# Third layer of a recurrent model: the readout turned back block by block inside the recurrence, and the last block in two halves

## The chip, the core and the metric

The kernel runs on one core of one Trainium2 chip. The metric is the device time of one execution in microseconds (us), as the median of several runs. A core has five engines that the profile names: PE (TensorE, the matrix engine, with PEld for its weight loads), DVE (VectorE), ACT (ScalarE), POOL (GpSimd) and SP (SyncE, which here only issues transfers). Each takes its instructions from a queue of its own, in the order in which the built kernel has them.

## The reference, cut to what matters

The model has four layers on 4 sequences of 256 tokens, 128 features wide. The change lies in the attention part of the third layer (index L2), a gated delta rule with a rotation: 16 heads, each with a state of 2 x 16. Beside it the same layer has a mixture of eight experts; the layer's output is x + attention + silu(experts).

```python
def step(S, inp):
    ct, st, kt, vt, bt = inp
    S0, S1 = (S[:, :, 0], S[:, :, 1])
    Sd = jnp.stack([ct[..., None] * S0 + st[..., None] * S1, -st[..., None] * S0 + ct[..., None] * S1], axis=2)
    pred = jnp.einsum('bhsd,bhd->bhs', Sd, kt)
    Sn = Sd + bt[:, :, None, None] * (vt - pred)[..., None] * kt[:, :, None, :]
    return (Sn, Sn)
...
_, Ys = jax.lax.scan(step, S0, xs)
Y = jnp.moveaxis(Ys, 0, 1)
retrieved = jnp.einsum('blhsd,blhd->blhs', Y, Q) * sel_C_gate[..., None]
y = retrieved.reshape(b, l, h * 2) @ readout_w
```

A group norm over the sequence, a silu gate and an output projection follow. The norm needs all 256 tokens of a sequence, so nothing behind it can begin before the last token's `retrieved`.

## The kernel before

**Layout.** The recurrence is computed without the rotation: keys and values are turned beforehand by the accumulated angle, so that a step only decays and updates, and what is read from the states is turned back afterwards with `cosp` and `sinp`. The partitions are state component x sequence x head (2 x 64 = 128 rows), and each row holds 16 numbers of state. The tokens come in NT = 8 blocks of 128 columns, each of NC = 16 chunks of CH = 8 tokens. Rows 0 to 63 and 64 to 127 are the two components of the same sequence and head.

**The recurrence** is the loop at the end of `scan2`: 128 steps n = 16 i + c (block i, chunk c), each four VectorE operations in a chain (L1664 product, L1667 sum, L1670 product, L1675 sum). A step gives the state at the chunk's end and the weights `w` of its 8 tokens. Every second step ScalarE copies two chunks' coefficients into the step's state tile (`bring`, L1644, three steps ahead); L1675 of a step waits for that copy.

**The states of all tokens** of a block are made from `w` by the generator `states(i, w)`, in six stages: load kt (SP); load qt, spread the decays into mz (L1601, ScalarE) and clear its first column; kt * w (L1606, POOL, with two small operations for the state carried in, L1611 and L1612); the scan over the block's tokens for 16 numbers at a time (L1615, VectorE, 128x2048), the copy of its last state for the next block (`last`, L1617, ScalarE) and the product with qt (L1618, POOL); 16 matmuls that sum over the 16 numbers (L1623, `read`, PE); the copy of the result to `o` (L1625, ScalarE). The tiles qt and mz exist once, kt twice.

**What sets the order.** The loop advances these generators by hand, after fixed chunks c: `turns` maps c to how many blocks back the advanced generator lies (c = 4 and 12 this block, c = 1 and 11 the block before, c = 3 and 7 the one before that). After the loop the last two generators are drained, so that the scan, the product and the reads of block 7 all stand behind the recurrence. After each step the loop also advances `beside`, the mixture of experts of the same layer (`experts2`): per sequence a router (L1068 to L1074), and per half of it eight experts, each with a gathered input `xs` (L1083, POOL), four transposes (L1090, PE), a copy `xin` (L1092, ScalarE), matmuls up (L1112) and down (L1101, L1102) with two ScalarE operations on `h` between (L1113, L1114), and a shared expert (L1122 to L1128); the result is turned (gT, L1130; PE's transposes in a helper at L125) and written out as `g` (L1134). The tile framework's scheduler then fixes each engine's order: it places every instruction into one queue per engine, so that expert work and recurrence work interleave in fixed order. Transposes take PSUM buffers of the tag "tr", which in this stage is the same as the experts' "mm" (three buffers).

**After the recurrence** `retrieve2` turns `o` (eight PE transposes, two 512-wide copies), multiplies and adds on 128x512 tiles (six VectorE and two POOL operations with cosp, sinp and outg, which is the gate sigmoid(sel_C) over |Q|), and transposes back to `retT`. `out2` then runs for the four sequences: 16 matmuls L1724 from retT, copies, statistics, the norm, the gate with sz (L1750, L1751) and the projection (L1760); it adds resid and g, loaded from DRAM by `layer2` (L1016, L1017).

**The gates** are computed by `gates2` before the recurrence: cosp and sinp, outg, and the coefficients, on 128x512 tiles on VectorE (`mul`, L1230) and POOL (`mulp`, L1231).

Of the kernel before, what the change touches and what calls it, by code (L numbers as in the profile page):

```python
# [10 lines left out]
F32 = mybir.dt.float32  # L11
# [4 lines left out]
ALU = mybir.AluOpType  # L16
AX = mybir.AxisListType
# [3 lines left out]
P = 128  # L21
NB = 4
T = 1024
NT = 8
# [906 lines left out]
def layer2(k, W, x_all, eps5, ps, banks, x3, whole, last, I, first):  # L931
# [4 lines left out]
    nc, tc = k.nc, k.tc  # L936
    tokens = lambda b: slice(b * NT, (b + 1) * NT)
    with tc.tile_pool(name="l2", bufs=1) as keep, tc.tile_pool(name="l2dram", bufs=1, space=DRAM) as dram:
        wide = lambda name: dram.tile([P, NB * NT, D], F32, tag=name, name=name)

        xd, rd, gd, xr = wide("xd"), wide("rd"), wide("gd"), wide("xr")
        szd = dram.tile([P, 2, NB * T], F32, tag="szd", name="szd")

        kd = dram.tile([NT, NB, 16, 16, P], F32, tag="kd", name="kd")
        qd = dram.tile([NT, NB, 16, 16, P], F32, tag="qd", name="qd")
        small = lambda name, shape=(P, 512): keep.tile(list(shape), F32, tag=name, name=name)
        cosp, sinp, outg = small("cosp"), small("sinp"), small("outg")
        coef = {name: small(name) for name in ("bias0", "bias1", "scale", "decay")}
        o = small("o", (P, T))
        late = ExitStack()  # L950
        with tc.tile_pool(name="l2g", bufs=1, side="right") as gp:
            raw = {
                "V": gp.tile([P, 32, 32], F32, tag="V", name="V"),
                "G": gp.tile([P, 7, 32, 16], F32, tag="G", name="G"),
                "N": gp.tile([P, 2, 32, 16], F32, tag="N", name="N"),
            }
            with tc.tile_pool(name="l2p", bufs=1) as p1, tc.tile_pool(name="l2pd", bufs=2) as p2:
                xn = p1.tile([P, NB * NT, D], F32, tag="xn", name="xn")

                def norm(b):  # L960

# [12 lines left out]
            banks.close()  # L974
            ps = PsumTags(banks, tc, {"mm": 3, "tr": "mm", "o": 2, "st": 2, "A": 1}, "ps2s")
            f1 = late.enter_context(tc.tile_pool(name="l2f", bufs=1))
            f2 = late.enter_context(tc.tile_pool(name="l2fd", bufs=2))
            experts = experts2(k, W, f1, f2, ps, xd, gd)
            early = {}
            with tc.tile_pool(name="l2m", bufs=1) as mp, tc.tile_pool(name="l2y", bufs=2) as yp:  # L980
                grams = grams2(k, f1, mp, yp, ps, kd, early)

                def beside():

                    while True:
# [12 lines left out]

        def behind_tables():
            room.close()  # L1000
            pre = room.enter_context(tc.tile_pool(name="l2pre", bufs=1, side="right"))
            for b in range(NB):
                szs.append(pre.tile([P, 2, T], F32, tag=f"sz{b}", name="sz"))
                nc.sync.dma_start(out=szs[b], in_=szd[:, :, b * T : (b + 1) * T])

        with late, tc.tile_pool(name="l2s1", bufs=1) as p1, tc.tile_pool(name="l2s", bufs=2) as p2, \
                tc.tile_pool(name="l2sd", bufs=2, space=DRAM) as dram2:
            scan2(k, p1, p2, ps, dram2, kd, qd, coef, o, experts, tp1, tp2, behind_tables, early)
        banks.close()
        ps = PsumTags(banks, tc, {"mm": 4, "tr": 2, "o": 2}, "ps2o")  # L1010
        with room, tc.tile_pool(name="l2o", bufs=NB) as p4, tc.tile_pool(name="l2x", bufs=2) as p2, \
                tc.tile_pool(name="l2r", bufs=1) as p1, tc.tile_pool(name="w3", bufs=1) as w3:
            parts = []
            for b in range(NB):
                resid, g = (p4.tile([P, NT, D], F32, tag=tag, name=tag) for tag in ("resid", "g"))
                nc.sync.dma_start(out=resid, in_=rd[:, tokens(b), :])  # L1016
                nc.sync.dma_start(out=g, in_=gd[:, tokens(b), :])  # L1017
                parts.append((resid, g))
            W3 = load3(k, w3, I)
            turned = prepare3(k, t3, W3, ps)  # L1020
            retT = p1.tile([P, T], F32, tag="retT", name="retT")
            retrieve2(k, p1, ps, o, cosp, sinp, outg, retT)
            done = []
            ends = [
                out2(k, W, p4, p2, ps, b, retT, szs[b], *parts[b], eps5, xr[:, tokens(b), :], x3[:, tokens(b), :], done)
                for b in range(NB)
            ]
            begin = None
            for n in range(2 * NB):
                for b in range(NB):  # L1030
                    if 0 <= n - b:
                        next(ends[b], None)
                        next(turned, None)
                        if done and begin is None:
                            begin = begin_first(k, W3, p1, ps, done[0], eps5, first)
                        if begin:
                            next(begin, None)
            drain(turned)
        return W3
# [182 lines left out]
def gates2(k, W, mp, ps, raw, cosp, sinp, outg, coef, beside, decays):  # L1222
# [152 lines left out]
    v.tensor_tensor(a1, a1, w, ALU.add)  # L1375
    mul(a0, a0, bv)
    mul(a1, a1, bv)

    for name, src in (("bias0", a0), ("bias1", a1)):
        k.transpose_tiles(ps, "tr", block(src), coef[name])  # L1380
# [166 lines left out]
        yield ktd, kdd  # L1547


def scan2(k, p1, p2, ps, dram, kd, qd, coef, o, beside, tp1, tp2, behind_tables, early):  # L1550

# [33 lines left out]
    def states(i, w):  # L1585
# [36 lines left out]
        for d in range(16):  # L1622
            nc.tensor.matmul(po, k.ident, hist[:, d, :], start=(d == 0), stop=(d == 15))  # L1623
        yield
        nc.scalar.copy(o[:, at], po)  # L1625
        yield

    def load(i):
        if i < NT:
# [17 lines left out]
            )  # L1647


    turns = {4: 0, 12: 0, 1: 1, 11: 1, 3: 2, 7: 2}  # L1650
    blocks, made_of = {}, {}
    load(0)
    bring(0)
# [1 line left out]
    for i in range(NT):  # L1655
# [4 lines left out]
        for c in range(NC):  # L1660
# [14 lines left out]
            v.tensor_reduce(then[:, 0:16, CH], step, AX.X, ALU.add)  # L1675
            next(beside, None)
            if c == 0:
                made_of[i] = states(i, w)
            if c in turns and i - turns[c] in made_of:
                next(made_of[i - turns[c]])  # L1680
            for _ in range(2 if i == 0 else 1):
                if len(made) < min(4, i + 3):
                    table()
# [5 lines left out]
    for i in (NT - 2, NT - 1):  # L1689
        drain(made_of[i])  # L1690
    drain(beside)


def retrieve2(k, p2, ps, o, cosp, sinp, outg, retT):

    nc = k.nc
    O = p2.tile([P, 8, 2, 64], F32, tag="O", name="O")
    k.transpose_tiles(ps, "tr", [o[:, (n % 2 * 4 + n // 2) * P :][:, 0:P] for n in range(NT)], O.rearrange("p a s c -> p (a s c)"))
    wide = lambda a: a.rearrange("p (a c) -> p a c", c=64)
    o0, o1 = O[:, :, 0, :], O[:, :, 1, :]  # L1700
    ret = p2.tile([P, 8, 64, 2], F32, tag="ret", name="ret")
    for s, (x, y, op) in enumerate(((o0, o1, ALU.add), (o1, o0, ALU.subtract))):
        a = p2.tile([P, 8, 64], F32, tag="a", name="a")
        u = p2.tile([P, 8, 64], F32, tag="u", name="u")
        nc.vector.tensor_tensor(a, x, wide(cosp), ALU.mult)
        nc.gpsimd.tensor_tensor(u, y, wide(sinp), ALU.mult)
        nc.vector.tensor_tensor(a, a, u, op)
        nc.vector.tensor_tensor(ret[:, :, :, s], a, wide(outg), ALU.mult)
    tiles = [ret[:, 2 * tt4 + half].rearrange("p c s -> p (c s)") for half in range(2) for tt4 in range(4)]
    k.transpose_tiles(ps, "tr", tiles, retT)  # L1710


def out2(k, W, p2, px, ps, b, retT, sz, resid, g, eps5, x_from, x_to, done):
# [680 lines left out]
```

## Time and profile before

| what | value |
|---|---|
| median of 3 runs | 3140.76 us (3139.37 to 3149.32) |
| the profiled execution | 3140.11 us, span 3138.4 us |
| granted TensorE clock, mean | 0.741 |
| busy, whole span | PE 69%, DVE 72%, ACT 50%, POOL 40% |
| the recurrence (L1664 to L1675) | 1652.1 to 1994.84 us |
| its last block, first step | 1967.01 us |
| experts' last ScalarE operation (g, L1134) | 1914.94 us |
| scans L1615, blocks 0 to 7, start | 1730.98, 1818.36, 1852.80, 1895.15, 1928.29, 1956.81, 1984.76, 1998.88 us |
| first product of `out2` (L1724) | 2024.59 us |

All times inside the profile are microseconds from the start of the span. A timeline line gives start, duration, engine, source line, operation, the tile written and the tiles read with their shapes, and in brackets how long the engine had been idle before and who released it. A waits line gives the instruction that waited, the one that it waited for, the total, how often and the longest. The windows view gives the busy time of each engine in each stretch. A source line can be that of a helper (L115, L117 and L125 are the copies and transposes of `transpose_tiles`).

### The profile page before, as it was taken

To read this page: it belongs to the slowest core of one execution; us is meant where nothing else is said; L and a number is where in the kernel's file an instruction comes from. 1 tells how busy PE (TensorE), PEld (TensorE's weight loads), DVE (VectorE), ACT (ScalarE), POOL (GpSimd) and SP (SyncE) were. 2 spreads that over 40 slices of the span, in tenths; PEclk is the share of its full clock that TensorE was granted. 3 is DMA by queue.
4 is the path that set the end of the run, shared out by engine and by line. 5 is a ranking of instruction groups with operands and counts; after the bars stand their busy time and mean duration, and the time that the engine had idled before them with its cause. 6 is when DMAs were issued, how large, how long until landed. Compare 5 with 4: busy or idle time off the path is not lost. (4 is left out here: it accounts for less than half of the span.)

```text
span 3138.4 us, 48108 instructions
## 1 busy us (share of the span) xinstructions
PE 2160.2 (69%) x17200; PEld 1281.2 (41%) x17201; DVE 2262.5 (72%) x5474; ACT 1565.8 (50%) x3350; POOL 1258.3 (40%) x1154
## 2 busy tenths in 40 slices
PE   5777777577777776794355474456777777877875
PEld 2555555333333232463122232344545544545553
DVE  5555555778888886665868977566788788698777
ACT  3554544333333333434354564136775866775773
POOL 3433434144433335225778853332233332323322
PEclk9888888588888887896555666675766676766666
DMA  3000000100000000222055365448678688678772
GB/s 78 17 1 1 1 1 1 36 0 0 0 0 0 7 7 7 94 96 66 0 143 131 95 175 127 121 134 281 182 240 276 179 261 262 206 239 275 220 246 66
DMA packets 334388, 335.26 MB, mean 107 GB/s; under 512 B 26032, under 2 KB 307500, under 8 KB 328260
## 3 DMA queue, kind: packets, MB, share of 16 engines
q1 hardware_dynamic: 332996, 328.00, 35.6%
q10 hardware_dynamic: 1152, 4.19, 0.4%
q8 instruction: 135, 2.21, 0.3%
q14 instruction: 105, 0.86, 0.1%
HBM read 177.40 MB, written 154.14 MB: 106 GB/s over the span
## 5 line engine op out<-in xcount | busy, mean ns | idle before, releaser
L2252 ACT ACTIVATE neg<-neg,low 128x640 f32<-128x640 f32 (+7 forms) x512 | 390.8, 766 | 102.5 <-DVE low L2245 101.5
L1939 DVE STREAM_TRANSPOSE wT<-neg 128x640 f32<-128x640 f32 (+7 forms) x512 | 366.1, 754 | 51.3 <-PE po L2266 47.7
L2196 POOL TENSOR_SCALAR_AFFINE_SELECT rel<-rel 128x512 f32<-128x512 f32 x288 | 179.8, 635 | 555.1 <-DMA rel<-flat 424.1
L2266 PE MATMUL po<-wT,vb 128*32 128x64 f32 (+1 forms) x10240 | 270.6, 256 | 71.5 <-issue 40.6
L2229 PE MATMUL score<-k,q 32*128 32x512 f32 (+3 forms) x768 | 225.4, 598 | 114.2 <-DVE low L2245 113.5
L2266 PEld LDWEIGHTS po<-wT,vb 128*32 128x32 f32 x10240 | 214.7, 137 | 144.4 <-issue 83.9
L2245 DVE CUSTOM_DVE_ANT_0 neg<-score,rel,low 128x128 f32<-128x128 f32 (+3 forms) x448 | 213.1, 510 | 74.1 <-PE score L2229 33.3
L2167 ACT COPY r<-pr 128x512 f32<-128x512 f32 x256 | 135.2, 584 | 137.9 <-PE pr L2165 96.2
L2245 DVE CUSTOM_DVE_ANT_0 neg<-score,rel 128x512 f32<-128x512 f32 (+3 forms) x320 | 150.7, 520 | 47.1 <-issue 23.2
L2229 PEld LDWEIGHTS score<-k,q 32*128 32x128 f32 x768 | 99.7, 252 | 205.1 <-DVE low L2245 132.8
L2165 PE MATMUL pr<-emb,q 32*128 32x256 f32 x512 | 128.6, 438 | 46.8 <-ACT r L2167 25.8
L840 ACT ACTIVATE h<-pg 128x512 f32<-128x512 f32 x128 | 75.9, 596 | 157.9 <-PE pg L837 154.4
L837 PE MATMUL pg<-xnT,w 128*128 128x512 f32 x256 | 149.3, 667 | 7.0 <-DVE h L841 3.9
L790 POOL TENSOR_TENSOR prod<-rest,kv 128x2048 f32<-128x2048 f32 x32 | 145.2, 4574 | 18.4 <-ACT rest L780 18.4
L839 PE MATMUL pu<-xin,w 128*128 128x512 f32 x256 | 140.6, 632 | 12.9 <-DVE h L841 7.4
L828 PE MATMUL po<-h,w 128*128 128x512 f32 x256 | 129.7, 627 | 26.3 <-DVE h L841 26.3
L2165 PEld LDWEIGHTS pr<-emb,q 32*128 32x128 f32 x512 | 92.3, 270 | 80.2 <-ACT r L2167 38.1
L433 PE MATMUL px<-hT,xbcT 128*128 128x512 f32 x256 | 115.1, 594 | 0.0
L785 DVE TENSOR_REDUCE s<-prod 128x128 f32<-128x2048 f32 x32 | 73.1, 2284 | 49.3 <-POOL prod L790 49.3
L1623 PE MATMUL read<-kt,const_sb 128*128 128x128 f32 x256 | 50.6, 369 | 82.7 <-POOL kt L1618 82.7
L2150 POOL COPY vb<-vr 32x1024 f32<-32x1024 f32 x64 | 66.5, 1040 | 79.8 <-PE po L2266 67.5
L1090 PE MATMUL pt<-ident,xs 128*128 128x128 bf16 x256 | 35.4, 290 | 90.7 <-POOL xs L1083 81.5
(648 smaller groups left out, 5849.4 us busy)
## 6 DMA issues: line engine op xcount, KB each, us to landing
flat<-r SPq DMA_DIRECT2D x128, 512.0 KB
rel<-flat SPq DMA_DIRECT2D x112, 512.0 KB
flat<-r SPq DMA_DIRECT2D x128, 256.0 KB
rel<-flat SPq DMA_DIRECT2D x96, 256.0 KB
kt<-kd SPq DMA_DIRECT2D x16, 512.0 KB
kdc<-kdd SPq DMA_DIRECT2D x16, 512.0 KB
qt<-qd SPq DMA_DIRECT2D x16, 512.0 KB
ktc<-ktd SPq DMA_DIRECT2D x16, 512.0 KB
```

Of the source, the lines that this page charges most:

```text
L790: nc.gpsimd.tensor_tensor(prod, attn.rearrange("p (t h g) -> p t h g", t=4, g=16)[:, t].unsqueeze(2).to_broadcast(each), kv[:, t, 1, :].re ...
L828: nc.tensor.matmul(po, W["w2"][:, e, c, :], h[:, c, :], start=(e == 0 and c == 0), stop=(e == 7 and c == 1))
L837: nc.tensor.matmul(pg, W["w1"][:, e, c * P : (c + 1) * P], xnT, start=True, stop=True)
L839: nc.tensor.matmul(pu, W["w3"][:, e, c * P : (c + 1) * P], xin, start=True, stop=True)
L1939: nc.vector.transpose(weights[at, pair][j][:, t % 2, 0 : (t + 1) * P], S[j][:, 0 : (t + 1) * P])
L2165: nc.tensor.matmul(to[:, m, :], q[at, t * P : (t + 1) * P], W["emb"][at, i, :], start=True, stop=True)
L2167: nc.scalar.copy(r[:, n], to)
L2196: nc.gpsimd.affine_select(out=rel[:, :, slot(back), :], in_=rel[:, :, slot(0), :], compare_op=op, fill=fill, base=0, pattern=[[0, 4], [-si ...
L2229: nc.tensor.matmul(halves[j // 2][:, j % 2, 0 : last - first], q[at(j), 1 + t * P : 1 + n], kk[at(j), first:last], start=True, stop=True)
L2245: nc.vector.tensor_tensor_reduce(out=neg[:, begin:last], in0=sc[:, begin - first : last - first], in1=rel[:, j, slot : slot + (last - begi ...
L2252: nc.scalar.activation(neg[:, 0:n], neg[:, 0:n], AF.Exp, bias=here, scale=-1.0, accum_out=group["sums"][:, j, t : t + 1])
L2266: nc.tensor.matmul(o[32 * j : 32 * j + 32, 2 * pair + m.start : 2 * pair + 2, :], vb[:, kb % 4 * NT + kb // 4, j].rearrange("p a d -> p (a ...
```

## The change

The block's output is no longer kept in `o`. After the reads of a block, five more stages follow in the same generator: `o` goes to a third of a tile of three 128x128 parts, PE turns it, VectorE multiplies by cosp and sinp (two 128x128 operations reading PSUM) and adds crosswise (two 128x64), PE turns the result back, and ScalarE copies it into the block's columns of retT. The factor outg is multiplied into cosp and sinp once, in `gates2`, on POOL. `retrieve2` is gone. `turns` becomes a list `usual` with nine entries, and for block 7 a list `at_end` with twelve.

Block 7 has its own generator, `last_states`: kt and qt are loaded in halves of 64 tokens (four transfers each, in pieces of 256 bytes); the first half is multiplied on POOL, scanned, multiplied with qt on POOL and summed by PE, all of it during the recurrence's last steps but for the sums; the second half is done on VectorE alone, with a sum over the 16 numbers in place of PE's matmuls.

```diff
@@ gates2
+    mulp(cosp, cosp, outg)
+    mulp(sinp, sinp, outg)
@@ scan2, states
-        nc.scalar.copy(o[:, at], po)
-        yield
+        three = room_for_three()
+        nc.scalar.copy(three[:, 0], po)
+        yield
+        yield from retrieve(i, three[:, 0], three)
+    def retrieve(i, o, three):
+        pt = ps.tile([P, 2, 64], F32, tag="tr", name="pt")
+        nc.tensor.transpose(pt.rearrange("p s c -> p (s c)"), o, k.ident)
+        yield
+        a = i % 4 * 2 + i // 4
+        both = lambda f: f[:, a * 64 : (a + 1) * 64].unsqueeze(1).to_broadcast([P, 2, 64])
+        y, ret = three[:, 1].rearrange("p (s c) -> p s c", s=2), three[:, 2].rearrange("p (c s) -> p s c", s=2)
+        k.tc.keep_in_program_order(v.tensor_tensor(ret, pt, both(cosg), ALU.mult))
+        v.tensor_tensor(y, pt, both(sing), ALU.mult)
+        v.tensor_tensor(ret[:, 0], ret[:, 0], y[:, 1], ALU.add)
+        v.tensor_tensor(ret[:, 1], ret[:, 1], y[:, 0], ALU.subtract)
+        yield
+        pt = ps.tile([P, P], F32, tag="tr", name="pt")
+        nc.tensor.transpose(pt, three[:, 2], k.ident)
+        nc.scalar.copy(retT[:, i * P : (i + 1) * P], pt)
+        yield
+    def last_states(i, w):
...
+        for dst, src in ((kt, kd), (qt, qd)):
+            for n in range(2):
+                for s in range(2):
+                    nc.sync.dma_start(
+                        out=dst[s * 64 : s * 64 + 64, n], in_=src[i].rearrange("b h d t -> (b h) d t")[:, :, n * H : (n + 1) * H]
+                    )
+        for n in range(2):
+            nc.scalar.copy(mz[:, n], m[:, i * P + n * H : i * P + (n + 1) * H].unsqueeze(1).to_broadcast([P, 16, H]))
+        nc.gpsimd.memset(mz[:, :, :, 0:1], 0.0)
+        yield
+        o = qt[:, 0].rearrange("p d t -> p (d t)")[:, 0:P]
+        for n, e in enumerate((nc.gpsimd, v)):
+            hist = kt[:, n]
...
+            e.tensor_tensor(more, last, m[:, first : first + 1].to_broadcast([P, 16]), ALU.mult)
+            e.tensor_tensor(hist[:, :, 0], hist[:, :, 0], more, ALU.add)
+            if n == 0:
+                yield
...
+            k.tc.keep_in_program_order(v.tensor_tensor_scan(flat(hist), flat(mz[:, n]), flat(hist), 0.0, ALU.mult, ALU.add))
+            if n == 0:
+                last = p2.tile([P, 16], F32, tag="last", name="last")
+                nc.scalar.copy(last, hist[:, :, H - 1])
+            e.tensor_tensor(hist, hist, qt[:, n], ALU.mult)
+            if n == 0:
+                yield
+                po = ps.tile([P, H], F32, tag="o", name="read")
+                for d in range(16):
+                    nc.tensor.matmul(po, k.ident, hist[:, d, :], start=(d == 0), stop=(d == 15))
+                nc.scalar.copy(o[:, 0:H], po)
+            else:
+                v.tensor_reduce(o[:, H:P], hist.rearrange("p d t -> p t d"), AX.X, ALU.add)
+        yield from retrieve(i, o, room_for_three())
@@ scan2, the loop
-    turns = {4: 0, 12: 0, 1: 1, 11: 1, 3: 2, 7: 2}
+    usual = ((1, 1), (3, 2), (4, 0), (7, 2), (9, 2), (11, 1), (11, 2), (12, 0), (14, 2))
+    at_end = ((1, 1), (2, 0), (3, 2), (7, 2), (8, 1), (9, 2), (10, 0), (11, 2), (12, 1), (13, 2), (13, 0), (14, 1))
...
-                made_of[i] = states(i, w)
-            if c in turns and i - turns[c] in made_of:
-                next(made_of[i - turns[c]])
+                made_of[i] = (last_states if i == NT - 1 else states)(i, w)
+            for turn, back in at_end if i == NT - 1 else usual:
+                if turn == c and i - back in made_of:
+                    next(made_of[i - back])
```

Each pair of `usual` and `at_end` is (chunk c, blocks back).

More of the change, by code (lines that the diff above doesn't have):

```diff
@@ L948, in layer2 @@
         coef = {name: small(name) for name in ("bias0", "bias1", "scale", "decay")}
-        o = small("o", (P, T))
+        retT = small("retT", (P, T))
         late = ExitStack()
@@ L1007, in layer2 @@
                 tc.tile_pool(name="l2sd", bufs=2, space=DRAM) as dram2:
-            scan2(k, p1, p2, ps, dram2, kd, qd, coef, o, experts, tp1, tp2, behind_tables, early)
+            scan2(k, p1, p2, ps, dram2, kd, qd, coef, cosp, sinp, retT, experts, tp1, tp2, behind_tables, early)
         banks.close()
@@ L1020, in layer2 @@
             turned = prepare3(k, t3, W3, ps)
-            retT = p1.tile([P, T], F32, tag="retT", name="retT")
-            retrieve2(k, p1, ps, o, cosp, sinp, outg, retT)
             done = []
@@ L1547, in chunks2, with scan2 @@
         yield ktd, kdd
-def scan2(k, p1, p2, ps, dram, kd, qd, coef, o, beside, tp1, tp2, behind_tables, early):
+def scan2(k, p1, p2, ps, dram, kd, qd, coef, cosg, sing, retT, beside, tp1, tp2, behind_tables, early):
     nc = k.nc
@@ L1624, in states, with room_for_three @@
         yield
-        nc.scalar.copy(o[:, at], po)
+        three = room_for_three()
+        nc.scalar.copy(three[:, 0], po)
         yield
+        yield from retrieve(i, three[:, 0], three)
+    def room_for_three():
+        return early["f1"].tile([P, NC * CH * (CH - 1) // 2], F32, tag="A", name="three")[:, 0 : 3 * P].rearrange("p (n c) -> p n c", c=P)
+    def retrieve(i, o, three):
[14 more added lines that the diff above has]
+        yield
@@ new lines, in last_states @@
+    def last_states(i, w):
+        nonlocal last
+        H = P // 2
+        halves = lambda a: a.rearrange("p d t -> p (d t)").rearrange("p (n d t) -> p n d t", n=2, t=H)
+        kt = halves(p2.tile([P, 16, P], F32, tag="kt", name="kt"))
+        qt = halves(p1.tile([P, 16, P], F32, tag="qt", name="qt"))
+        mz = halves(p1.tile([P, 16, P], F32, tag="mz", name="mz"))
+        for dst, src in ((kt, kd), (qt, qd)):
[11 more added lines that the diff above has]
+            hist = kt[:, n]
+            e.tensor_tensor(
+                hist.rearrange("p d (c t) -> p d c t", t=CH), hist.rearrange("p d (c t) -> p d c t", t=CH),
+                w[:, n * NC // 2 : (n + 1) * NC // 2, 0:CH].unsqueeze(1).to_broadcast([P, 16, NC // 2, CH]), ALU.mult,
+            )
+            more = p2.tile([P, 16], F32, tag="first", name="first")
+            first = i * P + n * H
+            e.tensor_tensor(more, last, m[:, first : first + 1].to_broadcast([P, 16]), ALU.mult)
+            e.tensor_tensor(hist[:, :, 0], hist[:, :, 0], more, ALU.add)
+            if n == 0:
+                yield
+            flat = lambda a: a.rearrange("p d t -> p (d t)")
+            k.tc.keep_in_program_order(v.tensor_tensor_scan(flat(hist), flat(mz[:, n]), flat(hist), 0.0, ALU.mult, ALU.add))
[12 more added lines that the diff above has]
+        yield from retrieve(i, o, room_for_three())
@@ L1691, in scan2 @@
     drain(beside)
[L1694 to L1710, printed above, removed]
 def out2(k, W, p2, px, ps, b, retT, sz, resid, g, eps5, x_from, x_to, done):
```

## The prediction

> **What bounds the kernel now.** The page's chain of the work that ended last names almost nothing here (issue 1%), so I went from the windows view of the third layer's recurrence (20 us a row) to the waits of each engine in it, and to the timeline. The recurrence starts at 1652.1 and its last step ends at 1994.84; the last block (block 7) starts at T0 = 1967.01.
>
> ```profile
> 1880.00:1900.00 20.00, 17.25 (x61) 5.69 (x59) 11.73 (x25) 19.80 (x41) 6.25 (x6) 0.67 0.38 77
> 1900.00:1920.00 20.00, 14.90 (x48) 8.26 (x46) 12.87 (x40) 8.53 (x20) 11.25 (x8) 0.68 0.57 143
> 1920.00:1940.00 20.00, 2.40 (x11) 2.40 (x12) 18.17 (x46) 4.18 (x10) 6.93 (x4) 0.58 0.53 113
> ```
>
> Columns: window, length, busy us of PE, PEld, DVE, ACT, POOL, granted clock, DMA share, GB/s. There are two regimes. From 1920 the recurrence runs at VectorE's pace (18.17 of 20 us, a step each 17.75/12 = 1.48 us). Until then VectorE idles and ScalarE is full with the experts. The waits between 1800 and 1930 say who holds whom:
>
> ```profile
> DVE st L1675 <- ACT st L1644: 20.7, 7, 5.6
> ...
> PE read L1623 <- POOL kt L1618: 10.9, 3, 4.1
> PE pt L1090 <- POOL xs L1083: 7.8, 2, 7.4
> ```
>
> The recurrence waits 20.7 us for its own `bring` copies (L1644), which stand in ScalarE's fixed order among expert work. The last such wait ends only when the experts do:
>
> ```profile
> 1914.94 0.60 ACT L1134 ACTIVATE g<-pt 128x512 f32<-128x512 f32 x1 [2.27 <-PE pt L125]
> 1915.93 0.38 ACT L1644 COPY st<-kdc 128x256 f32<-128x256 f32 x1 [0.40 <-ACT g L1134]
> ...
> 1916.34 0.31 DVE L1675 TENSOR_REDUCE st<-step 128x16 f32<-128x144 f32 x1 [4.08 <-ACT st L1644]
> ```
>
> So whatever delays the experts delays step 83 (of 128), and with it T0. Behind the recurrence stands a serial tail:
>
> ```profile
> 1984.76 4.42 DVE L1615 TENSOR_TENSOR_SCAN kt<-mz,kt 128x2048 f32<-128x2048 f32 x1
> ...
> 1998.88 4.43 DVE L1615 TENSOR_TENSOR_SCAN kt<-mz,kt 128x2048 f32<-128x2048 f32 x1 [4.03 <-POOL kt L1612]
> 2003.63 4.49 POOL L1618 TENSOR_TENSOR kt<-kt,qt 128x2048 f32<-128x2048 f32 x1 [4.79 <-ACT last L1617]
> 2008.18 5.56 PE L1623 MATMUL read<-kt,const_sb 128*128 128x128 f32 x32 [8.34 <-POOL kt L1618]
> 2014.09 1.09 PE L125 MATMUL pt<-const_sb,o 128*128 128x128 f32 x8 [0.36 <-ACT o L1625]
> 2016.17 0.69 DVE L1705 TENSOR_TENSOR a<-O,cosp 128x512 f32<-128x512 f32 x1
> 2022.72 1.94 PE L125 MATMUL pt<-const_sb,ret 128*128 128x128 f32 x8 [7.54 <-issue]
> ```
>
> One engine works at a time. `out2`'s first product (L1724) starts at 2024.59 = T0 + 57.6.
>
> **The change, part by part.**
>
> **1. The tail.** Gone: `retrieve2` (2014.09 to 2024.59, 10.5 us) and the full-width scan, product and sum of block 7. In the built order VectorE's new stream from T0 is: 9 steps (13.3), the scan of block 6 three steps earlier than before (4.4), so T0 + 17.7; 3 steps and the retrieval of block 5 (1.0, part 2), + 23.2; 2 steps and half a scan (4.42/2), + 28.4; 2 steps, the second half's product with w (1.19, L1751's unhindered 128x1024 row) and a small one (0.2), + 32.7; the retrieval of block 6 (1.0), a small one (0.2), half a scan (2.2), a product (1.2) and a sum over 16 x 64 (between L1513's 1.08 for 896 elements and half of L785's 2.28, so 1.2), + 38.5; last a transpose (0.5), four products (1.0), a transpose and a copy (0.8): T0 + 40.8. Beside it the first half: ScalarE's two mz copies (2.2, L1601's whole) now stand ahead of `last`, so POOL's product of block 6 runs from + 20.2 to + 24.7, PE reads it until + 30.3, turns it back behind VectorE's + 33.7, and then does 16 products of 64 columns, between 2.8 (half of 5.6) and 5.6, plus a copy of 0.3: + 37 to + 40. The later of the two joins decides; the first product of `out2` lies between + 40.8 and + 42.3. I take + 41.5, **-16.1 us**. The loads of resid and the weights are issued some 2 us before that instead of 11, but resid is first used at 2056, 31 us behind the first product, so they stay hidden; with that cover gone they would cost their 12 us.
>
> **2. Retrieval inside the recurrence.** Per block four VectorE operations: two 128x128 (0.28 each; L1531 has 0.276 for 112 wide) and two 128x64 (0.22): 1.0 us. Those of blocks 0 to 2 fall before step 83 and vanish in its wait; blocks 3 and 4 lie behind it in VectorE's own pace, **+2.0**; blocks 5 to 7 are in part 1. Two PE transposes and two ScalarE copies (0.27) a block cost nothing by themselves where PE is idle, after 1920 (2.40 of 20).
>
> **3. The new wait.** Before 1920 PE is not idle. In the built order the transpose back of block 0 stands in PE's queue behind the fifth expert's last product (ending 1807.1), ahead of three more experts and block 1's reads. It waits for VectorE's retrieval, which is placed behind the scan of block 1:
>
> ```profile
> 1807.03 0.61 PE L1090 MATMUL pt<-ident,xs 128*128 128x128 bf16 x4
> ...
> 1818.36 4.42 DVE L1615 TENSOR_TENSOR_SCAN kt<-mz,kt 128x2048 f32<-128x2048 f32 x1
> ...
> 1827.67 5.37 PE L1623 MATMUL read<-kt,const_sb 128*128 128x128 f32 x32 [4.09 <-POOL kt L1618]
> 1832.87 1.85 PE L1068 MATMUL pl<-gateT,xnT 128*128 128x8 f32 x16
> ```
>
> Scan end 1822.8 plus one operation of the next step and 1.0 us: PE resumes near 1824.4 instead of 1807.0, **17.4 us** later, and nobody else can feed the experts. Part comes back: before, PE stood idle for 4.09 us ahead of block 1's reads. Now these come first (1827.6, POOL unchanged), the three experts (1807.0 to 1818.5, 11.5, less the 1 us done before the reads) and the 5.4 us of reads end near 1843; transposes (2.0), the xnT copy (0.7) and transposes of gT (0.7) bring the router's L1068 to about 1847.5 instead of 1832.9: +14.7. From there the same work follows, bound by ScalarE (19.80 of 20), not by what PE could make up. At the end the coupling above hands it on: g at 1914.9 + 15, step 83 the same. VectorE alone would be at step 83 near 1903 (39 steps of 1.48 from 1824, two scans, about 12 us of expert and retrieval work and waits), so the wait does bind. Bounds: 0 if the experts regained it all, 17.4 plus about 10 if later blocks repeat it (rival B). I take **+15.0**.
>
> **4. The gates.** Two POOL products of 128x512 more (1.29 to 1.74 each, L1231). POOL idles 3.75 us before its L1083 at 1581.74, which covers them: 0, at most +3.5.
>
> **5. Block 7's loads in 256-byte pieces.** Before, its 1 MB of qt landed 5.7 us after issue. The x loads of the kernel's first 30 us took 9700 mixed packets in 0.556 of 16 engines' time, 27.5 ns each; 4096 pieces over 16 engines give 7.0 us (estimate). Issued at T0 + 24.7, the second half lands near + 33, and is needed at + 36: 0 now; twice that time per piece would make it + 40 and cost 3.6.
> The Trainium skill (DMA: Bandwidth & Descriptors, Specifications) speaks against this part: below 512 bytes a transfer becomes a read-modify-write and misses line rate; it gives no price, and the doubled time above would be such a case, 3144.6 instead of 3141.0. No row of before shows pieces of 256 bytes by themselves.
>
> One more row bears on part 1. POOL's product at 1989.50 to 1994.01 runs beside two-operand VectorE steps of 0.38 to 0.39, undisturbed, yet L1751 took 3.15 instead of 1.19 beside POOL at 2049.45. I cost it at 0, at most +2.
> The Trainium skill (SBUF — State Buffer, Who interferes with whom) has VectorE with two SBUF inputs and a reading GpSimd exclude each other for a whole instruction; by it, the first half's product on POOL would hold VectorE up to 2.3 us, 3143.3. The steps' rows disagree, L1751's agrees.
>
> **Sum** against the profiled execution's 3140.1 (span 3138.4; the median of the runs shown is 3140.8): -16.1 + 2.0 + 15.0 + 0 + 0 = +0.9, **3141.0 us**.
>
> **The rivals.**
> A, the experts regain it: the profile's 20.7 us of VectorE waits means slack somewhere, and ScalarE has no brings between expert operations in the stretch after the stall. Against: ScalarE is full at 19.80, and the last bring stands behind g. With only 3 us kept: 3140.1 - 16.1 + 2 + 3 = 3129.
> B, slower, by the same queue again: block 2's reads now stand after the third expert of the next half, and wait for POOL's L1618, which the built order puts behind block 3's L1606 (4.24). If scan 2 ends near 1862, the reads start near 1871 where PE would be ready near 1866, 5 us instead of the 3.85 of before; if block 3 adds as much and ScalarE's 19 expert operations ahead of one bring slow the scans that the reads wait for, the experts slip by 25, and the total is 3140.1 - 16.1 + 2 + 25 = 3151. It decides from a slip of 23.3 on.
> C, the halves gain nothing, because a load or the mz copies are late: py at T0 + 45 at worst, 3144.6; it ends within the band.
>
> **How the numbers follow.** Forecast with C 0.52, A 0.24, B 0.24. 0.3% is 9.4 us, about what a measurement of this kernel can tell from no change: faster is below 3131.4, slower above 3150.2, and each rival lies beyond its bound. The range reaches from just under A (3127) to just over B (3152), which also takes in the bounds of parts 1, 4 and 5 around the forecast.
>
> **What would show it.** PE idle from about 1807 to 1824 ahead of the transpose back; g's last ScalarE operation near 1930; step 83's wait there; T0 near 1984; the first `out2` product at T0 + 41.5. Wrong if PE doesn't stall there, if T0 moves under 7 us (A) or over 25 us (B), or if `out2` starts later than T0 + 46.

## The result and the profile after

The changed kernel takes 3154.99 us (median of 20 runs, 3144.20 to 3161.53) against 3142.36 us of the kernel before (20 runs, 3133.48 to 3151.18): ratio 1.0038, 95% interval 1.0028 to 1.0048. It is 0.4% slower. The forecast was 3141.0 in a range of 3127 to 3152, so it is 14 us off and outside the range. Some 2 us of that are the reference: the forecast was added to an execution of 3140.1 us, and the median of the 20 runs is 3142.4.

The profiled execution of the changed kernel took 3152.69 us (span 3151.0) against 3140.11 (3138.4). Its 12.6 us can be placed by four stretches between marks that both traces have:

| mark | before | after | difference | forecast |
|---|---|---|---|---|
| step 84, the first after the experts' end | 1916.69 | 1933.26 | +16.6 | +15.0 |
| from there to T0, the first step of block 7 | 50.32 | 58.84 | +8.5 | +2.0 |
| from T0 to the first product of `out2` | 57.58 | 44.12 | -13.5 | -16.1 |
| from there to the end of the span | 1113.8 | 1114.8 | +1.0 | 0 |
| sum | | | +12.6 | +0.9 |

Each of the four came out worse than forecast, the second by most. (T0 is the start of block 7's first step; the steps are counted from 0.) Line numbers of the changed kernel: steps L1736 to L1747, `bring` L1715, retrieval's transpose L1637, its VectorE operations L1642 to L1645, the transpose back L1648, experts' g L1132.

The wait that part 3 foretold is there. First PE's timeline of the changed kernel, then its waits between 1790 and 1960 (VectorE's and PE's):

```profile
1806.31 0.60 PE L1100 MATMUL po<-h,dnT 48*128 48x512 bf16 x1
1827.16 0.47 PE L1648 MATMUL pt<-const_sb,three 128*128 128x128 f32 x1 [20.26 <-DVE three L1645]
```
```profile
DVE st L1747 <- ACT st L1715: 30.4, 7, 11.3
...
PE pt L1648 <- DVE three L1645: 39.9, 2, 20.3
```

PE stands still for 20.3 us ahead of block 0's transpose back (forecast 17.4), and the recurrence's waits for `bring` grow from 21.7 us in the same stretch of the kernel before to 30.4 us. The second wait of the 39.9 falls after 1931, when the experts are done, and costs nothing. The end of the experts and the step that hangs on it, in ScalarE's and VectorE's timeline of the changed kernel:

```profile
1931.51 0.60 ACT L1132 ACTIVATE g<-pt 128x512 f32<-128x512 f32 x1 [2.27 <-PE pt L125]
...
1932.51 0.38 ACT L1715 COPY st<-kdc 128x256 f32<-128x256 f32 x1 [0.24 <-ACT retT L1649]
```
```profile
1932.91 0.31 DVE L1747 TENSOR_REDUCE st<-step 128x16 f32<-128x144 f32 x1 [1.94 <-ACT st L1715]
```

g comes 16.6 us late (1914.94 before), step 84 as well: the coupling held as told. What was not foretold is in VectorE's and GpSimd's timeline around the retrieval of block 3, here of the changed kernel:

```profile
1949.37 0.28 DVE L1643 TENSOR_TENSOR three<-pt,sinp 128x128 f32<-128x128 f32 x1
1949.86 4.32 DVE L1644 TENSOR_TENSOR three<-three 128x64 f32<-128x64 f32 x1
1954.11 0.25 DVE L1645 TENSOR_TENSOR three<-three 128x64 f32<-128x64 f32 x1
```
```profile
1949.60 4.51 POOL L1618 TENSOR_TENSOR kt<-kt,qt 128x2048 f32<-128x2048 f32 x1 [19.01 <-ACT last L1617]
1954.06 0.22 POOL L1611 TENSOR_TENSOR first<-last,m 128x16 f32<-128x16 f32 x1
```

A sum over 64 columns takes 4.32 us instead of 0.22. The profile shows no wait ahead of it: the time is in its duration, and it ends (1954.18) when GpSimd's product does (1954.11). The experiments below call this a lock. The same happens at 1822.62 (block 0) and 1982.23 (block 4), both 4.32 us.

The tail, VectorE, GpSimd and PE of the changed kernel (T0 = 1992.10):

```profile
2005.58 4.52 DVE L1615 TENSOR_TENSOR_SCAN kt<-mz,kt 128x2048 f32<-128x2048 f32 x1
...
2015.00 1.96 DVE L1644 TENSOR_TENSOR three<-three 128x64 f32<-128x64 f32 x1
...
2022.37 2.34 POOL L1688 TENSOR_TENSOR kt<-kt,qt 128x1024 f32<-128x1024 f32 x1 [5.02 <-DMA qt<-qd]
...
2027.09 6.45 PE L1693 MATMUL read<-kt,const_sb 128*128 128x64 f32 x32
...
2036.22 4.63 PE L1778 MATMUL py<-retT,ro 32*128 32x512 f32 x5 [0.35 <-ACT retT L1649]
```

The block's chain is as foretold; the reads of the half take 6.45 us, more than the upper end of 5.6, and VectorE lost another 1.7 us at 2015.00 in the same way as above. GpSimd's product with qt waits for the load and starts 0.7 us behind the half scan's end (2021.71).

### The profile page after: what moved, and what is told of

It reads as the page before. It is cut to its first block, busy times and chain, and to the rows that moved or that the text cites. A ratio compares the mean times of both kernels' runs of the same rounds, so it can differ in the third digit from the quotient of the medians.

```text
span 3151.0 us, 48156 instructions
## 1 busy us (share of the span) xinstructions
PE 2166.3 (69%) x17201; PEld 1282.4 (41%) x17201; DVE 2279.9 (72%) x5504; ACT 1567.2 (50%) x3354; POOL 1254.2 (40%) x1154
## 5 line engine op out<-in xcount | busy, mean ns | idle before, releaser
L1081 POOL TENSOR_TENSOR xs<-xn,score 128x512 bf16<-128x512 f32 x64 | 85.1, 1343 | 32.6 <-PE pt L1088 29.2
L841 DVE TENSOR_TENSOR h<-h,pu 128x512 f32<-128x512 f32 x128 | 85.4, 679 | 16.4 <-PE pu L839 7.8
```

## The experiments

The theory after the result: **two costs**. (1) PE's queue: block 0's transpose back stands ahead of three experts and waits for VectorE; the experts end late and the recurrence with them. (2) A lock: a VectorE operation with two operands in SBUF doesn't run beside a GpSimd product. The rivals stand in each expectation. Medians are of the run and of the kernel before beside it.

| run | this, us | before, us | ratio, 95% interval | step 84 | T0 | T0 to `out2` |
|---|---|---|---|---|---|---|
| changed kernel | 3154.99 | 3142.36 | 1.0038 (1.0028 to 1.0048) | +16.6 | +25.1 | 44.1 |
| sums from PSUM | 3142.98 | 3143.12 | 0.9997 (0.9986 to 1.0008) | +14.5 | +14.7 | 41.4 |
| transpose back later | 3146.16 | 3143.12 | 1.0011 (1.0001 to 1.0022) | +7.4 | +15.9 | 44.9 |
| both | 3135.84 | 3143.12 | 0.9974 (0.9964 to 0.9985) | +3.5 | +3.8 | 43.5 |
| whole last block | 3161.42 | 3143.12 | 1.0061 (1.0045 to 1.0076) | +16.6 | +25.2 | 53.8 |
| halves alone | 3133.14 | 3143.71 | 0.9964 (0.9951 to 0.9977) | +0.7 | +0.6 | 50.9 |
| later, and before the scan | 3134.12 | 3143.71 | 0.9963 (0.9950 to 0.9977) | -1.3 | -0.6 | 44.8 |
| both, later still | 3132.43 | 3143.71 | 0.9968 (0.9956 to 0.9980) | +4.7 | +4.9 | 41.6 |
| whole rows of qt | 3162.07 | 3143.71 | 1.0052 (1.0040 to 1.0064) | +17.7 | +26.2 | 45.7 |
| before the scan alone | 3141.07 | 3140.59 | 0.9994 (0.9975 to 1.0013) | +11.4 | +12.2 | 44.5 |
| all three | 3134.46 | 3140.59 | 0.9978 (0.9958 to 0.9997) | +5.2 | +5.8 | 43.6 |

The last three columns come from one profiled execution each, against that of before. Such an execution can lie a microsecond or more off from the start: step 0 came between 1.4 us earlier and 3.5 us later than before ("both, later still"), and from `out2` to the end it took 1108.8 to 1124.0 us in the different runs.

Nor does a difference of 3 us at step 84 say much. "Halves alone" has the instructions of the kernel before up to block 7, yet the last `g` but one (the operation that ends a half of the experts, L1134 in the kernel before) starts 3.0 us later in it (1883.51 instead of 1880.47), and step 84 0.7 us later. From that `g` to the last one it took 31.8 to 31.9 us in "sums from PSUM", "later, and before the scan" and "both, later still", 32.1 in "halves alone", and 34.5 to 35.4 in the eight others, before the change too. The granted TensorE clock in the last 7 us of this stretch was 0.90 to 1.00 in the first three, 0.76 in "halves alone" and 0.50 to 0.59 in the eight. The windows view of these 7 us, the kernel before and then "later, and before the scan" (the clock is the third number from the end):

```profile
1907.94:1914.94 7.00, 7.00 (x20) 3.97 (x19) 3.88 (x12) 0.59 (x2) 5.70 (x6) 0.50 0.70 150
```
```profile
1906.63:1913.63 7.00, 4.55 (x23) 2.75 (x23) 4.13 (x14) 3.31 (x9) 7.00 (x4) 1.00 0.84 197
```

So some 3 us of the column "step 84" go with the clock that the execution happened to get there, and not with an edit.

**Sums from PSUM.**

```diff
-        pt = ps.tile([P, 2, 64], F32, tag="tr", name="pt")
+        pt = ps.tile([P, 4, 64], F32, tag="tr", name="pt")
...
-        y, ret = three[:, 1].rearrange("p (s c) -> p s c", s=2), three[:, 2].rearrange("p (c s) -> p s c", s=2)
+        y, ret = pt[:, 2:4], three[:, 2].rearrange("p (c s) -> p s c", s=2)
...
```

> One edit to the changed kernel: the product with sinp (y) is kept in PSUM instead of SBUF, so that the two cross-wise sums of the retrieval read one operand from SBUF and one from PSUM; everything else, PE's order too, is as in the changed kernel (3155 us, step 84 of the recurrence 16.6 us later than before, block 7 25.1 us later). Theory (two costs: PE's wait for the retrieval holds up the experts, and a sum with two SBUF operands beside GpSimd's product is held until that product ends): the first sum takes 0.22 us in every block instead of 4.32 in blocks 0, 3 and 4; block 7 starts 8.2 us earlier for blocks 3 and 4 and some 4 us earlier because PE's wait for block 0 ends 4.1 us sooner, so its shift falls from 25 to about 13 us, and the total to about 3142. Rival (the 4.3 us belong to the sum itself, to its stride or to the wait for its operand, not to GpSimd): the sum stays at 4.3 us in the same blocks, 3155.

The view of that line over the whole kernel (count, then minimum, median and maximum duration in ns):

```profile
L1644 DVE TENSOR_TENSOR three<-three,pt x8: 208/216/221, 1822.6 to 2021.9; 128x64 f32<-128x64 f32 x8
```

All eight sums take 0.21 to 0.22 us with one operand in PSUM. T0 comes 10.4 us earlier than in the changed kernel, of which 8.3 lie between step 84 and T0 (blocks 3 and 4). The 2.1 in front of it are not the lock's: PE's wait for block 0 is 16.1 instead of 20.3 us, but the router behind it (L1066) starts at 1844.54, in the changed kernel at 1844.48, and the last `g` but one at 1896.43 and 1896.85; the gain comes only behind that, where the clock differs. The expected 4 us from the shorter wait are not there. The tail is 41.4 us, the forecast's 41.5. The rival falls; 3143.0 against 3142 expected.

**Transpose back later.**

```diff
-    usual = ((1, 1), (3, 2), (4, 0), (7, 2), (9, 2), (11, 1), (11, 2), (12, 0), (14, 2))
-    at_end = ((1, 1), (2, 0), ...
+    usual = ((1, 1), (2, 3), (3, 2), (4, 0), (7, 2), (9, 2), (11, 1), (11, 2), (12, 0))
+    at_end = ((2, 3), (1, 1), (2, 0), ...
```

> One edit to the changed kernel: the stage that turns a block's result back is advanced at chunk 2 of the following block (three blocks back) instead of chunk 14, in block 7 too; PE's queue then has block 0's transpose behind the last expert of the half instead of behind the fifth. Theory: PE's 20 us wait ahead of that transpose goes, the experts end within 3 us of where they ended before the change (1914.9), step 84 shifts by under 4 us instead of 16.6, the lock on the sums of blocks 3 and 4 (8.2 us) stays: total about 3155 - 13 = 3142. Rival (the experts are late because the retrieval takes one of three PSUM buffers and VectorE time from them, wherever the transpose stands): step 84 stays over 10 us late, total 3149 or more.

The wait ahead of the sixth expert is gone, step 84 comes 9.2 us earlier than in the changed kernel, the lock stays in blocks 3 and 4 (4.33 us each). But step 84 is 7.4 us late, not under 4, and the total is 3146.2 instead of 3142: a miss, and the rival's bound of 10 isn't reached either. A part of what is left is told under "all three".

**Both.**

> The edits of the first two runs together: the second factor in PSUM, and the transpose back advanced at chunk 2 of the following block. Theory: the costs are separate and both go; left are one microsecond of VectorE per block behind step 84 and the tail's 13.5 us of gain: block 7 starts 2 to 5 us later than before, total 3142 - 13.5 + 4 = 3132, faster than before by 0.3%. If the two are one cost seen twice: 3142, no better than either edit alone.

T0 is 3.8 us late, the total 3135.8 against 3132: the two costs are separate, and each edit takes its own. The tail is 43.5 us instead of 41.4, with reads of the half of 7.1 us instead of 5.1 (why is told in the next section). This kernel is 0.3% faster than before.

**Whole last block** (the halves undone).

```diff
-                made_of[i] = (last_states if i == NT - 1 else states)(i, w)
-            for turn, back in at_end if i == NT - 1 else usual:
+                made_of[i] = states(i, w)
+            for turn, back in usual:
```

> The changed kernel with the last block treated like the others (the generator of the other blocks, the usual list of turns in block 7 too): the retrieval inside the recurrence alone. Theory: block 7 starts where it does in the changed kernel (25 us later than before), and the tail is that of before less retrieve2's 10.5 us plus one block's retrieval of 2.3: the first out2 product at T0 + 49.4 instead of T0 + 44.1, total 3155 + 5 = 3160. Rival (the halves bring nothing, since loads in 256-byte pieces, copies and the sums on VectorE eat them): within 2 us of 3155.

T0 is the changed kernel's, the total 6.4 us more (5 expected). The tail is 53.8 instead of 44.1, longer than the expected 49.4: here the sums of blocks 5 and 6 are held too (4.32 us at 2015.07, 1.57 at 2027.04). The halves gain, though by the medians alone the two intervals still touch; the next run shows it from the other side.

**Halves alone** (the kernel before with `last_states` writing into `o`, `retrieve2` kept).

```diff
-    turns = {4: 0, 12: 0, 1: 1, 11: 1, 3: 2, 7: 2}
+    usual = ((1, 1), (3, 2), (4, 0), (7, 2), (11, 1), (12, 0))
+    at_end = ((1, 1), (2, 0), (3, 2), (7, 2), (8, 1), (10, 0), (12, 1), (13, 0), (14, 1))
```

> The kernel before with the last block in two halves alone: last_states and the list at_end for block 7 are put in, o and retrieve2 stay, no retrieval runs inside the recurrence. Theory: the experts and T0 stay where they were before (no PE wait, no lock: within 1 us), and the tail is the changed kernel's 44.1 us without its last retrieval (2.3) and without the retrievals of blocks 5 and 6 with their lock (some 4), plus retrieve2's 10.5: the first out2 product near T0 + 48 instead of T0 + 57.6, total 3143 - 9 = 3134. Rival (the halves are paid for elsewhere, by late loads or by VectorE doing the sums): within 3 us of 3143.

Step 84 and T0 stay (0.7 and 0.6 us), the tail is 50.9 (48 expected): 6.1 us earlier into `out2`. The total is 10.6 us less (9 expected); the profile places 6.1 of them, and the rest isn't found (this profiled execution was the slowest of the five, with 1124.0 us behind `out2`).

**Before the scan.** The retrieval's VectorE stage at chunk 10, ahead of the scan whose end starts GpSimd's product; once with the transpose back later, once alone. The first, as an edit to "transpose back later":

```diff
-    usual = ((1, 1), (2, 3), (3, 2), (4, 0), (7, 2), (9, 2), (11, 1), (11, 2), (12, 0))
+    usual = ((1, 1), (2, 3), (3, 2), (4, 0), (7, 2), (9, 2), (10, 2), (11, 1), (12, 0))
```

> The run with the later transpose back, with one more move: the retrieval's VectorE stage is advanced at chunk 10, ahead of the next block's scan, instead of behind it at chunk 11; both operands of the sums stay in SBUF. Theory (the sum is held by GpSimd's product, which starts when the scan ends): with two SBUF operands but no product beside it, the sums of blocks 0 to 4 take 0.22 us, as they did with one operand in PSUM; block 7 is 8 us earlier than with the later transpose alone (15.9 us late there), and the total near 3136 to 3138. Rival (two SBUF operands are slow by themselves in this shape): the sum stays at 4.3 us wherever it stands, 3146.

The view of the sum's line in this run:

```profile
L1644 DVE TENSOR_TENSOR three<-three x8: 210/217/1962, 1816.2 to 2009.9; 128x64 f32<-128x64 f32 x8
```

Both operands are in SBUF as in the changed kernel, and all but one take 0.22 us; the one of 1.96 is block 5's, in block 7, where the list `at_end` still puts it beside the product. So neither the shape nor two operands in SBUF make the sum slow by themselves; it takes GpSimd's product beside them, and by "sums from PSUM" one operand in PSUM is enough to be free of it. Step 84 and T0 are 1.3 and 0.6 us earlier than before the change, where 8 us late was expected for T0. The last `g` but one is still 1.3 us late. Of the 8.6 us by which step 84 is earlier than with the later transpose alone, 3.5 lie behind that `g`, where the clock differs (1.00 and 0.51); the other 5.1 lie in front of it, and "all three" tells a part of them.

The same stage alone, with the transpose back left where the changed kernel has it:

> One edit to the changed kernel: the retrieval's VectorE stage is advanced at chunk 10, ahead of the next block's scan, instead of at chunk 11 behind it; the transpose back stays at chunk 14, so that PE still waits for the retrieval ahead of the sixth expert, but for less time: VectorE gives block 0's sums near 1816 instead of 1827, so PE's wait is about 10 us instead of 20.3. Theory: step 84 comes 16.6 - 10 = 6 to 8 us late instead of 16.6, the sums run beside no product (0.22 us instead of 4.32, 8.5 us less in blocks 3 and 4), block 7 starts 6 to 9 us late instead of 25, total 3155 - 17 = 3138. Rival (the experts' delay doesn't follow from the length of PE's wait): step 84 still 14 us or more late, total 3146.

The changed kernel's PE order with a shorter wait. PE's timeline in this run:

```profile
1816.45 0.48 PE L1648 MATMUL pt<-const_sb,three 128*128 128x128 f32 x1 [8.96 <-DVE three L1645]
...
1820.33 0.60 PE L1100 MATMUL po<-h,dnT 48*128 48x512 bf16 x1
1826.58 2.50 PE L1623 MATMUL read<-kt,const_sb 128*128 128x128 f32 x10 [5.64 <-POOL kt L1618]
```

The wait is 9.0 us, yet step 84 is still 11.4 us late, not 6 to 8, and the total 3141.1 instead of 3138: the expectation's size was wrong. The next thing in PE's queue, block 1's reads, stands ahead of the last two experts as well and waits 5.6 us for GpSimd. That is rival B's mechanism, at an earlier block than B had it. Before the change PE also waited there (4.1 us), but with no expert of that half behind.

**All three.**

> The changed kernel with all three edits: second factor in PSUM, VectorE stage ahead of the scan, transpose back at chunk 2 of the following block. Theory: nothing is left of PE's wait or of the lock, block 7 starts within 1 us of before, as with the second and third edit alone, and the tail is the 41.5 us that the factor in PSUM gave instead of 44.8: total 3134 - 3 = 3131, 0.4% faster than before. If PSUM and the earlier stage only do the same thing, 3134.

T0 is 5.8 us late, not within 1 us, and the total 3134.5 instead of 3131. Step 84 is 5.2 us late where "later, and before the scan" has -1.3, with the same turns. PE is a microsecond later here from 1804 on; then the two traces part at one instruction, the shared expert's product on GpSimd (L1122); first this run, then "later, and before the scan":

```profile
1817.04 4.45 DVE L1615 TENSOR_TENSOR_SCAN kt<-mz,kt 128x2048 f32<-128x2048 f32 x1
1817.38 0.59 ACT L1121 ACTIVATE hs<-ph 48x512 f32<-48x512 f32 x1 [1.00 <-PE ph L1120]
...
1818.05 4.28 POOL L1122 TENSOR_TENSOR hs<-hs 48x512 f32<-48x512 f32 x1 [0.83 <-ACT hs L1121]
...
1822.38 2.07 PE L1126 MATMUL po<-hs,sdnT 48*128 48x512 f32 x2 [1.96 <-POOL hs L1122]
```
```profile
1816.82 1.03 POOL L1122 TENSOR_TENSOR hs<-hs 48x512 f32<-48x512 f32 x1 [0.62 <-ACT hs L1121]
```

The scan has two operands in SBUF too. Where the product on GpSimd comes after the scan's start it takes 3.3 us longer, and the shared expert on PE (L1126) ends at 1824.45 instead of 1819.03; where it comes half a microsecond ahead of the scan it isn't held. In the run with the transpose back later the product took 4.28 us too and PE waited 3.3 us for it, which is part of that run's 7.4. Of each kernel there is one execution, so how often either order comes isn't known, and by the medians (0.9978 and 0.9963, intervals overlapping) "all three" isn't shown to be slower.

**Both, later still** (chunk 6 instead of 2).

> The two edits together (second factor in PSUM, transpose back later) with the transpose back advanced at chunk 6 of the following block instead of chunk 2, so that it also stands behind the transposes of gT, for which it cost PE 4.19 us. Theory: the experts end 1 to 2 us later than before the change instead of 3.5, block 7 starts about 2 us late instead of 3.8, total 3134. If the remaining 3.5 us come from the PSUM buffer that the retrieval holds, nothing moves: 3136.

From step 0 (3.45 us late in this execution) step 84 loses 1.3 us, T0 1.4, against 3.9 and 4.2 in "both". But up to the last `g` but one it loses 2.6 against 3.4, and the rest goes with the clock (0.90 here, 0.57 there). The median is 3.4 us lower, but the intervals overlap: no gain is shown.

**Whole rows of qt.**

```diff
...
+        for s in range(2):
+            fetch2(nc, qt[s * 64 : s * 64 + 64], qd, i)
...
-            e.tensor_tensor(hist, hist, qt[:, n], ALU.mult)
+            e.tensor_tensor(hist, hist, qt[:, :, n * H : (n + 1) * H], ALU.mult)
```

> The changed kernel with qt of block 7 loaded in whole rows of 8 KB (two transfers, as in the other blocks) instead of four transfers in pieces of 256 bytes; its two halves are read as strided views, and the block's output goes to a part of mz instead of qt. Theory: the pieces took 7.7 us of the queue's time for 1 MB, but the first half of qt held the product on GpSimd by only 0.6 us and the second half arrived in time, so at most 1 us is won: 3154 to 3155. Rival (pieces under 512 bytes are what the tail lost): the tail shortens by the 2.6 us that it missed the forecast by, 3152.

Not faster (3162.1, where 3154 to 3155 was expected and 3152 by the rival): 1.0052 against the changed kernel's 1.0038, intervals overlapping. The tail is 1.6 us longer: the first half's product waits for all of qt and starts 2.4 us behind the scan instead of 0.7.

## Why the prediction was wrong

**What failed first: the row beside part 5, and with it part 2 ("+2.0").** I saw VectorE's steps run at 0.38 us beside GpSimd's 4.5-us product, called them two-operand operations, and costed the company at "0, at most +2". But those steps read `st`, which `scan2` allocates from the PSUM pool: they have one operand in SBUF. The retrieval's sums have two. Of the two rows that I had, L1751's (3.15 instead of 1.19) was the one of the right kind: both its operands are in SBUF. VectorE and GpSimd of the kernel before, first a step beside the product, then L1751:

```profile
1989.50 4.51 POOL L1618 TENSOR_TENSOR kt<-kt,qt 128x2048 f32<-128x2048 f32 x1 [18.61 <-ACT last L1617]
...
1992.00 0.38 DVE L1664 TENSOR_TENSOR prod<-ktc,st 128x136 f32<-128x136 f32 x1
...
2049.18 2.34 POOL L1750 TENSOR_TENSOR y<-y,sz 128x1024 f32<-128x1024 f32 x1
2049.45 3.15 DVE L1751 TENSOR_TENSOR y<-y,sz 128x1024 f32<-128x1024 f32 x1 [1.41 <-ACT y L1749]
```

The Trainium skill (SBUF — State Buffer, Who interferes with whom) states just this, two inputs in SBUF against a GpSimd instruction that reads SBUF; the trace agrees with it (4.32 us ending with the product, 0.22 from PSUM, 0.22 without the product), and my objection from the steps' rows was no objection. The term that the sum put at 0 measured 8.3 us in part 2 alone: +8.5 between step 84 and T0 in the changed kernel, +0.2 with the sums from PSUM (forecast +2.0; a wait of 0.94 us that stood there before, at 1944.87, is gone). It also made PE's wait 4.1 us longer (20.3 instead of 16.1), which cost the experts nothing that the traces show, and took part of the tail. With the sums from PSUM alone, and PE's wait still there, the kernel takes 3143.0 us, which is in the forecast's range.

**Part 3, PE's new wait: the mechanism right, the size near by luck.** +16.6 instead of +15.0; the run without it is down to +7.4, and in every run step 84 moves with g, within 1.3 us. Its place and its way through `bring` are as told. But the sum had the router behind the wait 14.7 us late, and it was 11.6 (1844.48 instead of 1832.87); from there, where the sum had the same work follow, another 4.8 us were lost up to the last `g` but one (1896.85 instead of 1880.47). In that stretch PE waits 3.5 us for an expert's input from GpSimd (at 1860.61, beside block 2's scan) and 5.4 us instead of 3.9 ahead of block 2's reads, which is what rival B had; how the 4.8 us divide wasn't tested. Nor was it told that block 1's reads come to hold the last two experts when the first wait is shortened, so that shortening it gives back only part.

**Part 1, the tail: -13.5 instead of -16.1.** Two things cost here. The lock (1.7 us on a sum, 0.5 on the product with w) made the reads of the first half start at T0 + 35.0, against 33.4 to 33.7 in the runs with the sums from PSUM. And the reads themselves took 6.45 us, where the sum had 2.8 to 5.6 because their products have half the columns. In the runs they took between 3.9 us ("both, later still") and 7.2 us ("all three"), and the granted TensorE clock during them was 1.00 and 0.50; time times clock is 3.5 to 3.9 us in every run, and as much for 16 products of 128 columns (5.55 us at 0.67 in the tail before). So half the columns saved nothing. Meeting the forecast's 41.5 with the lock off was luck: "sums from PSUM" (41.4) and "both, later still" (41.6) had clocks of 0.74 and 1.00 there, while "both" and "all three", at 0.51 and 0.50, had 43.5 and 43.6. The sum over 16 x 64 on VectorE took 1.89 us instead of 1.2, which other terms made up for.

**Part 4, the gates at 0:** step 0 is 0.75 us earlier, within what step 0 varies by. **Part 5, the small pieces at 0:** 1 MB in 4160 packets took 0.427 of 18 us, 7.7 us (forecast 7.0), 29.6 ns each, and held the first half's product by 0.7 us. The Trainium skill says (DMA: Bandwidth & Descriptors, Specifications) that pieces under 512 bytes miss the line rate; that is borne out by 7.7 against 4.7 us for whole rows, but not as a cost of this change. The part looked at the second half only. With the lock off the half scan ends sooner, and the first half's load then holds GpSimd's product for 2.6 us ("sums from PSUM" and "both"); whether that lengthens the tail wasn't tested.

**The loads behind the tail** stayed hidden, as told: from the first `out2` product to the first output projection it is 26.4 us, 27.0 before.

**The rivals.** A is out. B named the right sign and about the right total (3151), but by a slip of the experts of 25 us; they slipped by 16.6. The total reached B's region by the lock, which the list of rivals didn't have; T0 moved by 25.1 us, just past the 25 that were to speak for B, but 8.3 of them are the lock. (By its own sum B decides from a slip of 24.2 us, 3150.2 less 3126.0, and not from 23.3.) The range was too narrow because it gave the lock 2 us at most.

**Open:** why "halves alone" gains 10.6 us where its profile places 6.1; and whether retrieval in the recurrence, mended, gains anything on top of the halves. By the marks it should (`out2` starts at 2011.2 instead of 2018.5), by the medians it doesn't (3134.1 and 3133.1).

## What to carry to other kernels

Before you put small operations beside a long one on the neighbour engine, look up where each operand lives: a row prices another operation only if both have the same kind of operands. A transpose or copy that waits for another engine holds everything behind it in its queue, so read in the built order who stands behind it, and move its issue to a place where the result is long there. When two parts of a change come together, measure them apart: here the halves alone gained 0.4%, and the retrieval alone cost 0.6%. And before you give a few microseconds of one execution to an edit, look at the granted clock of that stretch.

## What the runs showed of the hardware

- A VectorE operation with two SBUF operands beside a reading GpSimd product shows no wait in the profile; it shows a long duration (0.22 us becomes 4.32). With one operand in PSUM it took 0.21 to 0.22 us beside the same product. It works both ways: GpSimd's product of 1.03 us became 4.28 behind the start of VectorE's scan.
- PE's float32 sums of 16 products took as long with 64 columns as with 128 at the same granted clock: 6.45 us at 0.55, 5.06 at 0.74 and 3.85 at 1.00 with 64, 6.65 at 0.55 and 5.17 at 0.73 with 128. In the changed kernel weight loads (PEld) were busy for 6.25 of the 6.45 us.
- Four transfers with 256-byte pieces kept SP busy issuing for 3.3 to 3.5 us, two with whole rows for 1.1.
